# Channel gate of the last image computed from sums inside its last two products, and the first product ahead of the fifth logits

## The chip, the cores and the metric

The kernel runs on one core of one Trainium2 chip. The metric is the device time of one execution in microseconds (us), from the start of the program on the core to its end; of several executions the median is taken. All arithmetic is in float32.

## The reference

The input is x, 16 images of 256 channels and 28x28 pixels. Each image is group-normalised, run through two layers that stand in for 3x3 convolutions, gated per channel, and added to what came in:

```python
def amm_conv3x3(x, centroids, w_sub):
    p = patches of 3x3, per pixel and channel 9 values          # B, HoWo, C, 9
    d = |p|^2 - 2 p.centroids + |centroids|^2                   # 16 centroids a channel
    attn = softmax(-d)                                          # over the 16
    lut = einsum('cks,cso->cko', centroids, w_sub)
    return einsum('bnck,cko->bno', attn, lut)

def se_layer(x, w1, b1, w2, b2):
    s = mean(x, axis=(2, 3))
    s = relu(s @ w1 + b1)
    s = sigmoid(s @ w2 + b2)
    return x * s

xn = groupnorm(x, 32 groups)
out = relu(batchnorm(amm_conv3x3(xn, centroids1, wsub1)))
out = batchnorm(amm_conv3x3(out, centroids2, wsub2))
out = se_layer(out, se_w1, se_b1, se_w2, se_b2)
return x + relu(out + xn)
```

The gate of an image (`se_layer`) needs the mean of each of its 256 output channels over all 784 pixels, so it needs the whole of the second layer's output for that image.

## The kernel before

**Tiling.** Channels lie on the 128 partitions, in two halves. The pixels of an image are cut into two halves of 392 columns (`N`). A block is one layer, one image, one half of the input channels and one half of the pixels: 2 x 16 x 4 = 128 blocks. Each block loads its patches (`patches`, SyncE's queue), multiplies them with the centroids into PSUM (`logits`, 64 matrix products), takes exponentials on ScalarE (`exps`), multiplies these with the centroids' values (`num_b`, which also gives the softmax's denominators, then `num_a`), and scales by the reciprocal denominators (`recip_dve`, `spread`, `scale_a` on VectorE, `scale_q` on GpSimd). What is left per block are nine operands q of 128x392 that meet nine 128x128 weight matrices.

**Products.** The four blocks of an image would need eight products of nine matrices each (two input halves, two output halves, two pixel halves). As in Strassen's scheme they are combined into seven: `PRODUCTS` lists them by the cluster in which they run, `mix` (GpSimd) forms the differences of operands, `combine` those of weights. One product is one call of `product`, nine matrix products of 128x128 by 128x392, each of which the trace shows as two instructions. The outputs land in the regions c11, c12, c21 and c22 (output half, pixel half) by `acc_copy`, `acc_add` and `reg_add`. In image order the products carry the numbers 5 to 12; those that matter here are 9 to 12 of the last image. Product 11 is needed by c11 alone, product 12 by c21 alone.

**Order.** No scheduler sets the order. Every call is entered in a table by `at(cluster, sub, function, ...)`, and the program is recorded in the order of the sorted keys; each engine then runs its instructions in that order and waits where an operand or a buffer is not ready. In the table g is 8 times the number of the image within the two layers (0 to 31, so the second layer's last image has n = 31); a key like (g + 11, 1.9) is a place in the eleventh cluster after that image's first. Blocks overlap: while one block's products run, the next ones' logits, exponentials and scalings run.

**PSUM.** A ring of four tiles of two banks each (tags ps0 to ps3, `banks`, `bank`) serves everything. Which tag a tile gets follows from its step and a role (`ROLES`); for the first blocks a table overrides it (`EARLY`), and a call without step goes round robin. A new tile waits until the last reader of the tile with the same tag is done.

**The start.** Image 0's second half of channels and image 1's normalisation run among the first blocks. Product 5 of image 0 (`acc`, weights w_A) is split: at sub 0.8 five of its nine matrices, then the group means of image 1 (`gn_mean`), two matrices, the group variances (`gn_var`), two matrices. All four logits groups of block 2 stand around it. Image 1 arrives in one transfer (`load_x`).

**The end.** After the last product c21 is formed (`acc_add`), scaled and summed by channel (`norm_out`, ScalarE with an accumulator); then the gate: `se_hidden` (four matrix products, two ScalarE operations), `se_gate` (one matrix product, three ScalarE operations), `se_recip` (VectorE); then `finish_fast` per channel half (two VectorE passes of 784 columns) and `store` (SyncE's queue). `flags` checks, with nine small VectorE operations, that the softmax stayed in range, `flag_sum` adds the flags up on TensorE, and every engine loads the sum at the end; were it above zero, a slower fallback (the loop under `tc.If`) would redo everything. It is not run here. The second last image's gate and output (`finish_gate`, `finish_sum`, `finish_relu`, `finish_add`) run on ScalarE and GpSimd beside the last image's products.

Of the kernel before, what the change touches and what calls it, by code (L numbers as in the profile page):

```python
# [55 lines left out]
    "acc": {4: 0, 6: 1, 7: 3}, "small": {4: 1},  # L56
# [28 lines left out]
def kernel(  # L85
# [83 lines left out]

    def load_x(b, spare=False):  # L170
        if spare:
            t = epool.tile([P, 4, N], F32, tag="e", name="e").rearrange("p i n -> p (i n)")
            t = t.rearrange("p (b n) -> p b n", b=NB)
# [5 lines left out]
    def load_x0(k):  # L179
        if k == 0:  # L180
            xs[0] = io.tile([P, NB, HW], F32, tag="xt", name="xt")
        nc.sync.dma_start(xs[0][:, k], x[0, k * P : (k + 1) * P])

    load_x0(0)
# [46 lines left out]
    load_x0(1)  # L231
# [67 lines left out]
    def small_bank(name, step):  # L299
        return bank(name, step, step and ROLES["small"][step % 2], EARLY["small"].get(step))  # L300
# [42 lines left out]
    def gn_mean(b, k0=0, n=NB, step=None):  # L343
        st, mv = gst[b]
        ps = small_bank("gnp", step)[:, : 2 * n]
# [14 lines left out]
    def gn_var(b, k0=0, n=NB, step=None):  # L360
        gm, dv = gst.pop((b, "m"))
        ps = small_bank("gnp", step)[:, :n]
# [186 lines left out]
    def product(key, us, w, ks, first=True, last=True, step=None):  # L549
        if first:  # L550
            accs[key] = bank("acc", step, step and ROLES["acc"][step % 2], EARLY["acc"].get(step))
        for n, k in enumerate(ks):
            nc.tensor.matmul(  # L553
                accs[key][:, :N], lhsT=wl[w][:, k, :], rhs=us["q", k],
                start=first and n == 0, stop=last and n == len(ks) - 1,
            )
# [282 lines left out]
    def se_hidden(b, step=None):  # L839
        ysum = ys[b, "sum"]  # L840
        ps = small_bank("sep", step)[: 2 * RED, :1]
        terms = [(k, i) for k in range(NB) for i in range(2 if b >= B - 1 else 1)]
        for k, i in terms:
            nc.tensor.matmul(  # L844
                ps, lhsT=w1_sb[:, k, :], rhs=ysum[:, k, i : i + 1],
                start=(k, i) == terms[0], stop=(k, i) == terms[-1],
            )
# [5 lines left out]
    def se_gate(b, step=None):  # L853
        ps = small_bank("sep", step)[:, :NB]
# [16 lines left out]
    def finish_norm(b, k):  # L871
        if k == 0:
            if b == B - 1:
                ys[b, "t"] = epool.tile([P, 4, N], F32, tag="e", name="xn").rearrange("p i n -> p (i n)")
# [25 lines left out]

    def store(b, k, dst=None, eng=None):
# [22 lines left out]
    def flag_sum():  # L924
        ps = bank("flp")[:, :1]
# [76 lines left out]

    for l in range(2):
        for b in range(B):
# [3 lines left out]
            for c, w, r, ks in PRODUCTS:  # L1008
                if g + c == 5:
                    for sub, k0, k1 in ((0.8, 0, 5), (0.82, 5, 7), (0.84, 7, 9)):  # L1010
                        at(4, sub, product, (n, c), us[r], w, ks[k0:k1], k0 == 0, k1 == 9, step=4)
                else:
                    at(g + c, 1.32 if g + c == 7 else 2.0, product, (n, c), us[r], w, ks, step=g + c)
            for mm in (1, 2, 3, 4, 0):
# [3 lines left out]
                at(g + 10, 1.4, mix, us[0], mm, us[0], us[3])  # L1018
# [10 lines left out]
            at(g + 12, 0.0, acc_add, l, b, c11, (n, 11))  # L1029
            at(g + 12, 2.02, acc_add, l, b, c21, (n, 12), op=ALU.subtract)  # L1030
            if l == 0 or b == B - 1:
                at(g + 11, 1.9, norm_out, l, b, *c12)
                at(g + 11, 1.91, norm_out, l, b, *c22)
                at(g + 12, 1.9 if l else 0.05, norm_out, l, b, *c11)
                at(g + 13, 1.06, norm_out, l, b, *c21)
            else:
                for o in range(NB):
                    at(g + 12 + o, 1.9, norm_both, b, o)
            if l == 0:
# [8 lines left out]
                if b + 1 < B:  # L1048
                    at(*((g - 2 + (b == 1), 2.6 - (b == 1)) if b else (0, 1.65)), load_x, b + 1)
                    for q in range(NB):  # L1050
                        at(*(((g + 1, 1.5) if b == 1 else (g, 0.3)) if b else (3, 1.3)), gn_stats, b + 1, q)
                    at(*((g + 1, 2.1) if b else (4, 0.81)), gn_mean, b + 1, step=g + 1 if b else 4)
                    at(*((g + 3, 2.1) if b else (4, 0.83)), gn_var, b + 1, step=g + 3 if b else 4)
                    for q in range(NB):
                        at(*((g + 4, 1.9) if b else (4, (0.95, 1.055)[q])), gn_apply, b + 1, q)
                        at(*((g + 4, 1.92) if b else (4 + 3 * q, 1.6 + 0.05 * q)), to_home1, b + 1, q)
            else:
                last = b == B - 1
                at(*((g + 11, 0.6) if last else (g + 13, 2.6)), load_x, b, last)
                at(g + 14 - last, 2.1, se_hidden, b, g + 14 - last)  # L1060
                at(*((g + 14, 1.05, se_gate, b, g + 14) if last else (g + 17, 2.1, se_gate, b, g + 17)))
                at(*((g + 14, 1.05) if last else (g + 18, 0.3)), se_recip, b)
                for q in range(NB):
                    at(*((g + 12, 0.4) if last else (g + 19, 1.9)), finish_norm, b, q)
                    if not last:
# [5 lines left out]
                    else:  # L1071
# [254 lines left out]
```

## Time and profile before

| what | us |
|---|---|
| median of three runs | 2622.44 |
| lowest and highest of them | 2621.93, 2623.15 |
| the profiled execution | 2621.02 |
| its span from first to last instruction | 2619.5 |
| TensorE busy in it | 2583.4 |
| mean granted TensorE clock (1 is full speed) | 0.998 |

The profile is of one more execution. Its times are counted from the start of its span, which is some 1.5 us shorter than the time of that execution. PE is TensorE, DVE VectorE, ACT ScalarE, POOL GpSimd, SP SyncE. A row of a timeline gives start, duration, engine, line, operation, tile written and read, shapes and the number of instructions; in brackets, where there is one, the idle time of the engine before it and what ended that.

### The profile page before, as it was taken

How to read it: one execution, taken by the hardware profiler on the slowest of the kernel's cores; microseconds unless marked ns; L12 is line 12 of the kernel's file. 1: busy time of each engine (PE TensorE's matmuls, PEld its weight loads, DVE VectorE, ACT ScalarE, POOL GpSimd, SP SyncE). 2: the span in 40 equal slices, each digit the busy share in tenths (PEclk: the TensorE clock that was granted, in tenths of full speed). 3: DMA queues.
4: the chain of work that ended last, by engine and by line, in shares of the span. 5: the costliest groups of instructions: out<-in, count | busy, mean ns of one | idle time of the engine just before them, and what ended most of it. 6: DMA issues, size and time to landing. Idle time of an engine off the chain costs nothing.

```text
span 2619.5 us, 85666 instructions
## 1 busy us (share of the span) xinstructions
PE 2583.4 (99%) x36984; PEld 1265.0 (48%) x36984; DVE 1761.6 (67%) x3759; ACT 1360.3 (52%) x1879; POOL 1900.5 (73%) x1316
## 2 busy tenths in 40 slices
PE   6999999999999999999999999999999999999997
PEld 2444454444444444444444444444444444444444
DVE  5776656666566665566676767766776767677665
ACT  5444544444444454444445555555555556555553
POOL 3786666766568766677666887878878778878786
PEclk9999999999999999999999999999999999999999
DMA  8556656655555566554664444444444443444441
GB/s 223 157 162 180 196 152 188 169 170 173 155 144 148 168 184 178 166 166 135 179 168 103 112 109 129 119 122 119 103 118 128 126 117 104 117 123 121 117 121 45
DMA packets 217959, 374.37 MB, mean 143 GB/s; under 512 B 29752, under 2 KB 188520, under 8 KB 217576
## 3 DMA queue, kind: packets, MB, share of 16 engines
q1 hardware_dynamic: 211256, 335.24, 48.1%
q0 software_dynamic: 6320, 33.58, 3.6%
q8 instruction: 295, 4.83, 0.8%
q14 instruction: 88, 0.72, 0.1%
HBM read 288.93 MB, written 79.80 MB: 141 GB/s over the span
## 4 chain that ended last, share of the span: by engine, by line
PE 97%; DMA 1%; DVE 1%; POOL 0%; ACT 0%; SPq 0%; issue 0%; DVEq 0%; POOLq 0%; ACTq 0%
PE acc L553 52%; PE lg L418 17%; PE na L469 14%; PE nb L483 14%; DMA wall<-home 0%; DMA pt<-home 0%; PE sep L855 0%; DVE r L511 0%; SPq L404 0%; ACT e L429 0%; POOL qp L562 0%; PE sep L844 0%; DMA home<-xpad 0%; DMA xt<-in_x 0%; DVE rb L526 0%
## 5 line engine op out<-in xcount | busy, mean ns | idle before, releaser
L553 PE MATMUL acc<-qp,wall 128*128 128x392 f32 x3072 | 1096.8, 500 | 0.9 <-DVE qp L545 0.7
L429 ACT ACTIVATE e<-lg 128x784 f32<-128x784 f32 x960 | 737.9, 820 | 635.1 <-PE lg L418 632.2
L562 POOL TENSOR_TENSOR qp<-qp,qp 128x784 f32<-128x784 f32 x512 | 943.5, 1867 | 155.6 <-DVE qp L545 155.1
L553 PEld LDWEIGHTS acc<-qp,wall 128*128 128x128 f32 x3072 | 566.4, 190 | 507.1 <-issue 56.9
L526 DVE STREAM_SHUFFLE rb<-r 128x392 f32<-128x392 f32 x1024 | 551.0, 604 | 0.0
L418 PE MATMUL lg<-pt,wd 32*32 32x392 f32 x16256 | 483.2, 502 | 7.2 <-DMA wall<-home 4.9
L497 DVE SCALAR_TENSOR_TENSOR r<-nb,kst,r 128x392 f32<-128x392 f32 x128 | 80.1, 626 | 458.6 <-ACT r L493 444.1
L545 DVE TENSOR_TENSOR qp<-na,rb 128x784 f32<-128x784 f32 x352 | 333.8, 972 | 59.4 <-PE na L469 48.2
L483 PE MATMUL nb<-e,cwb 64*32 64x392 f32 x8192 | 373.6, 492 | 0.1
L469 PE MATMUL na<-e,cwa 64*32 64x392 f32 x8192 | 373.7, 492 | 0.0
L534 POOL TENSOR_TENSOR qo<-qo,rb 128x392 f32<-128x392 f32 x128 | 132.5, 1035 | 310.2 <-DVE rb L522 309.4
L511 DVE RECIPROCAL r<-r 128x392 f32<-128x392 f32 x128 | 333.2, 2603 | 4.4
L534 POOL TENSOR_TENSOR qp<-qp,rb 128x784 f32<-128x784 f32 x160 | 295.8, 1858 | 3.2 <-ACT hpad L604 0.4
L483 PEld LDWEIGHTS nb<-e,cwb 64*32 64x32 f32 x8192 | 189.5, 107 | 176.6 <-issue 20.8
L469 PEld LDWEIGHTS na<-e,cwa 64*32 64x32 f32 x8192 | 182.2, 106 | 182.4 <-issue 72.9
L418 PEld LDWEIGHTS lg<-pt,wd 32*32 32x32 f32 x16256 | 120.9, 103 | 281.8 <-issue 243.1
L553 PE MATMUL acc<-qp,w_A 128*128 128x392 f32 x512 | 182.7, 499 | 0.0
L493 ACT ACTIVATE r<-nb,kst 128x392 f32<-128x392 f32 x128 | 86.7, 678 | 162.3 <-PE nb L483 162.3
L453 POOL TENSOR_TENSOR z<-z,mx 128x1568 f32<-128x1568 f32 x32 | 91.8, 2869 | 94.8 <-DVE mx L447 94.8
L553 PE MATMUL acc<-qo,wall 128*128 128x392 f32 x384 | 157.8, 493 | 0.0
L539 ACT COPY qp<-na 128x784 f32<-128x784 f32 x160 | 130.0, 812 | 26.2 <-PE na L469 24.4
L553 PEld LDWEIGHTS acc<-qp,w_A 128*128 128x128 f32 x512 | 94.7, 190 | 82.1 <-DVE qp L545 19.8
(159 smaller groups left out, 1642.8 us busy)
## 6 DMA issues: line engine op xcount, KB each, us to landing
pt<-home SPq DMA_DIRECT2D x762, 209.0 KB
pt<-home SPq DMA_DIRECT2D x762, 104.5 KB
home<-xpad SPq DMA_DIRECT2D x30, 899.0 KB
xt<-in_x SPq DMA_DIRECT2D x30, 784.0 KB
out_dram<-y SPq DMA_DIRECT2D x32, 392.0 KB
d_wS<-st SPq DMA_DIRECT2D x12, 192.0 KB
wall<-d_wS SPq DMA_DIRECT2D x4, 576.0 KB
wall<-in_ws SPq DMA_DIRECT2D x3, 576.0 KB
```

What stands on the lines that cost most here:

```text
L418: nc.tensor.matmul(bk[32 * c : 32 * c + 32, :N].rearrange("p (r w) -> p r w", w=W), lhsT=wts["wd", u["hh"]][32 * i : 32 * i + 32, mm, c, : ...
L429: nc.scalar.activation(eg[:, 2 * i : 2 * i + 2, :], bk[:, :, :N], AF.Exp, scale=2.0)
L453: nc.gpsimd.tensor_tensor(zk, zk, mx.unsqueeze(2).to_broadcast([P, N // 4, K]), ALU.subtract)
L469: nc.tensor.matmul(bs[32 * i : 32 * i + 32, r, :N], lhsT=wts["cwa", u["hh"]][64 * r : 64 * r + 64, mm, i, :], rhs=es[64 * r : 64 * r + 64, ...
L483: nc.tensor.matmul(bs[32 * i : 32 * i + 32, r, :N], lhsT=wts["cwb", u["hh"]][64 * r : 64 * r + 64, mm, i, :], rhs=es[64 * r : 64 * r + 64, ...
L511: nc.vector.reciprocal(u["r"], u["r"])
L526: nc.vector.stream_shuffle(rb[:, r, :], u["r"], mask_of(2 * mm + r))
L534: nc.gpsimd.tensor_tensor(q, q, u.pop(("rb", mm)), ALU.mult)
L539: nc.scalar.copy(pair(u, mm), u.pop(("na", mm))[:, :, :N])
L545: nc.vector.tensor_mul(pair(u, mm), u.pop(("na", mm))[:, :, :N], rb)
L553: nc.tensor.matmul(accs[key][:, :N], lhsT=wl[w][:, k, :], rhs=us["q", k], start=first and n == 0, stop=last and n == len(ks) - 1,)
L562: nc.gpsimd.tensor_tensor(pair(out_u, mm), pair(in0, mm), pair(in1, mm), ALU.subtract)
```

## The change

It has an end part and a start part.

**End, the gate.** The channel sums of the last image that still depend on products 11 and 12 are no longer taken from the products' outputs. A product's sum over columns is the weights times the operands' sums, so `total_act` (ScalarE, accumulators) and `total_dve` (VectorE) sum the nine operands, `total_sub` takes the difference, `weigh` multiplies the eighteen weight matrices of A12 and A22 by these sums (ScalarE, written with a step of nine elements), `weigh_sum` adds them over the nine (VectorE), and `rest_sum` adds over the partitions (two matrix products with one column) and multiplies by the batch norm's scale. `se_hidden` gets two more terms from it. Product 11 is split 5 / 2 / 2 with `rest_sum`, then `se_hidden` and `flag_sum`, between its parts, and `se_gate` follows it, ahead of product 12.

**End, the last product.** Product 12 runs as two halves of 196 columns, in two PSUM tiles (tags 2 and 3). Everything but its contribution is finished beforehand: `norm_join` and `finish_part` for c11, c12 and c22, `finish_ahead` for c21. Each half is then finished by two VectorE operations on 196 columns (`finish_last`) and stored at once, the second from ScalarE's queue.

**End, the second last image.** Its gate and sum run on ScalarE into PSUM tile ps3 (`gate_wide`) and in two VectorE operations (`finish_wide`); its GpSimd and second ScalarE pass fall away. Image 15's x is loaded earlier and normalised earlier, into the patch tile pt0, which is free by then.

**Start.** Five matrices of product 5 move ahead of block 2's first logits, in a new order (`KO1`). Image 1 arrives by halves of its channels, and each half has its own statistics, group means and group variances: the first half's at the old places, the second half's after block 2.

```diff
-    ("lg", 2): ((1, 0), (3, 2), (3, 2), (1, 0)), ("nb", 2): 3, ("na", 2): (0, 2, 3, 1),
+    ("lg", 2): ((1, 2), (3, 1), (3, 2), (1, 0)), ("nb", 2): 3, ("na", 2): (0, 2, 3, 1),
...
+KO1 = (2, 3, 4, 5, 8, 0, 1, 6, 7)
...
+    def gate_wide(b, k):
+        ys[b, "g"] = banks("gp", tag=3)[:, :, :N]
+        y = ys[b, k].rearrange("p (t n) -> p t n", t=2)
+        nc.scalar.activation(ys[b, "g"], y, AF.Copy, scale=se[b][:, k : k + 1])
...
+    def total_act(u, k):
+        nc.scalar.activation(
+            spare_of(NB * S * P, N, 1), u["q", k], AF.Identity, bias=zero, scale=one, accum_out=qsum[:, 1, k : k + 1]
+        )
...
+    def weigh(o, ks):
+        for k in ks:
+            nc.scalar.activation(
+                spare_of(o * S * P, S * P, 1).rearrange("p (n k) -> p n k", k=S)[:, :, k], wl["A22" if o else "A12"][:, k, :], AF.Copy, scale=qsum[:, o, k : k + 1]
+            )
+
+    def weigh_sum(o):
+        v = spare_of(o * S * P, S * P, 1).rearrange("p (n k) -> p n k", k=S)
+        nc.vector.tensor_reduce(vsum[:, o, :], v, axis=AX.X, op=ALU.add)
+
+    def rest_sum(b, tag):
+        ps = bank("pv", tag=tag)[:, :NB]
+        for o in range(NB):
+            nc.tensor.matmul(ps[:, o : o + 1], lhsT=vsum[:, o, :], rhs=one, start=True, stop=True)
+        ys[b, "rest"] = rest[:, 1]
+        nc.vector.tensor_tensor(rest[:, 1], ps, rest[:, 0], ALU.mult)
...
+    def finish_last(b, key, n0, n1):
+        y, x0 = ys[b, 1][:, n0:n1], xs[b][:, 1, n0:n1]
+        t = ys[b, "t"][:, HW + n0 : HW + n1]
+        nc.vector.scalar_tensor_tensor(
+            y, accs.pop(key)[:, : n1 - n0], rest[:, 2, 1:2], t, op0=ALU.mult, op1=ALU.add
+        )
+        nc.vector.scalar_tensor_tensor(y, y, 0.0, x0, op0=ALU.max, op1=ALU.add)
...
     def flag_sum():
-        ps = bank("flp")[:, :1]
+        ps = bank("flp", tag=2)[:, :1]
...
-                    for sub, k0, k1 in ((0.8, 0, 5), (0.82, 5, 7), (0.84, 7, 9)):
-                        at(4, sub, product, (n, c), us[r], w, ks[k0:k1], k0 == 0, k1 == 9, step=4)
+                    for sub, k0, k1 in ((0.05, 0, 5), (0.8, 5, 7), (0.82, 7, 9)):
+                        at(4, sub, product, (n, c), us[r], w, KO1[k0:k1], k0 == 0, k1 == 9, step=4)
+                elif n == 2 * B - 1 and c == 11:
+                    for sub, k0, k1 in ((1.95, 0, 5), (1.97, 5, 7), (1.99, 7, 9)):
+                        at(g + c, sub, product, (n, c), us[r], w, ks[k0:k1], k0 == 0, k1 == 9, tag=0)
...
+                elif n == 2 * B - 1 and c == 12:
+                    at(g + c, 1.99, open_last, n)
+                    for h in range(2):
+                        at(g + c, 2.0 + 0.02 * h, product, (n, 12 + h), us[r], w, ks, cols=(N // 2 * h, N // 2 * h + N // 2))
...
+                at(g + 11, 1.96, rest_sum, b, 1)
+                at(g + 11, 1.98, se_hidden, b, None, 1)
+                at(g + 11, 1.995, se_gate, b, None, 1)
...
-                    at(g + 11, 1.9, flags)
-                    at(g + 12, 2.9, flag_sum)
+                    at(g + 11, 1.962, flags)
+                    at(g + 11, 1.985, flag_sum)
```

TensorE, the first product and the logits of block 2, before:

```order
13 L483 MATMUL nb<-e,cwb_151 32x392 x32
14 L418 MATMUL lg<-pt_168,wd_153 32x392 x32
15 L553 MATMUL acc<-qp_175,w_A_141 128x392 x2
16 L553 MATMUL acc<-qp_176,w_A_141 128x392 x2
17 L553 MATMUL acc<-qp_177,w_A_141 128x392
18 L346 MATMUL gnp<-gn_mv,gmat 128x4
19 L553 MATMUL acc<-qp_177,w_A_141 128x392
20 L553 MATMUL acc<-qo_186,w_A_141 128x392
21 L363 MATMUL gnp<-gn_dv,gmat 128x2
22 L553 MATMUL acc<-qp_174,w_A_141 128x392 x2
```

The same place after:

```order
13 L486 MATMUL nb<-e,cwb_151 32x392 x32
14 L556 MATMUL acc<-qp_175,w_A_141 128x392 x2
15 L556 MATMUL acc<-qp_176,w_A_141 128x392 x2
16 L556 MATMUL acc<-qo_186,w_A_141 128x392
17 L421 MATMUL lg<-pt_168,wd_153 32x392 x32
18 L556 MATMUL acc<-qp_174,w_A_141 128x392 x2
19 L349 MATMUL gnp<-gn_mv,gmat 128x2
20 L556 MATMUL acc<-qp_177,w_A_141 128x392 x2
21 L366 MATMUL gnp<-gn_dv,gmat 128x1
```

The logits now stand behind five of the product's matrices, and the two `gnp` products carry one channel half each; those of the second half stand some rows further on, around the first quarter of the next `num_a`.

VectorE, the flags and what follows them, before (`ok`, `fl` and `csum` belong to `flags`, `y<-acc,y` and `y<-y,acc` are `acc_add` of products 11 and 12):

```order
1706 L914 TENSOR_SCALAR ok<-wsum 128x128
1707 L915 TENSOR_SCALAR ok<-wsum 128x128
1708 L916 TENSOR_REDUCE fl<-ok 128x1
1709 L917 TENSOR_SCALAR fl<-fl 128x1
1710 L918 TENSOR_SCALAR csum<-csum 128x2
1711 L919 TENSOR_REDUCE fl<-csum 128x1
1712 L920 TENSOR_SCALAR fl<-fl 128x1
1713 L921 TENSOR_TENSOR fl<-fl 128x1
1714 L922 MEMSET fl 128x1
1715 L590 TENSOR_TENSOR y<-acc,y 128x392
1716 L592 TENSOR_TENSOR y<-y,acc 128x392
1717 L927 COPY fi<-flp 1x1
```

The same place after, behind the two `weigh_sum` and the second part of `rest_sum`:

```order
1722 L1015 TENSOR_SCALAR ok<-wsum 128x128
1723 L1016 TENSOR_SCALAR ok<-wsum 128x128
1724 L1017 TENSOR_REDUCE fl<-ok 128x1
1725 L1018 TENSOR_SCALAR fl<-fl 128x1
1726 L1019 TENSOR_SCALAR csum<-csum 128x2
1727 L1020 TENSOR_REDUCE fl<-csum 128x1
1728 L1021 TENSOR_SCALAR fl<-fl 128x1
1729 L1022 TENSOR_TENSOR fl<-fl 128x1
1730 L1023 MEMSET fl 128x1
1731 L911 TENSOR_TENSOR gp<-gp,xn 128x2x392
1732 L912 TENSOR_SCALAR y<-gp,xt 128x784
1733 L1028 COPY fi<-flp 1x1
```

Between the flags and the copy of their sum (`fi<-flp`) now stands the second half of the second last image's `finish_wide` (`gp<-gp,xn` and `y<-gp,xt`), and the `acc_add` of products 11 and 12 are gone; `norm_join`, `finish_part`, `finish_ahead` and `finish_last` follow.

TensorE at the end, after (`pv` is `rest_sum`, `sep` the gate; before, products 11 and 12 were whole and the gate stood behind both):

```order
1947 L556 MATMUL acc<-qp_180,wall_140 128x392
1948 L954 MATMUL pv<-one,pt_169 128x1 x2
1949 L556 MATMUL acc<-qp_180,wall_140 128x392
1950 L556 MATMUL acc<-qo_188,wall_140 128x392
1951 L849 MATMUL sep<-ysum,w_sb 32x1 x4
1952 L849 MATMUL sep<-rest,w_sb 32x1 x2
1953 L1027 MATMUL flp<-fl 1x1
1954 L556 MATMUL acc<-qp_181,wall_140 128x392 x2
1955 L857 MATMUL sep<-se_hh,w_sb 128x2
1956 L556 MATMUL acc<-qp_182,wall_140 128x196 x2
```

The row `flp<-fl` puts the flag sum inside product 11, and the first half of product 12 (128x196) goes into the PSUM tile that `flp` used.

More of the change, by code (lines that the diff above doesn't have):

```diff
@@ L297, with small_bank @@
     cst = const.tile([P, 64], F32, name="cst")
-    def small_bank(name, step):
-        return bank(name, step, step and ROLES["small"][step % 2], EARLY["small"].get(step))
+    def small_bank(name, step, tag=None):
+        return bank(name, step, step and ROLES["small"][step % 2], EARLY["small"].get(step) if tag is None else tag)
     def center_sq(wf, c0, w, eng=None):
@@ L837, with se_hidden @@
     se = {}
-    def se_hidden(b, step=None):
+    def se_hidden(b, step=None, tag=None):
         ysum = ys[b, "sum"]
[L841 to L847, printed above, removed]
+        ps = small_bank("sep", step, tag)[: 2 * RED, :1]
+        terms = [(k, ysum[:, k, i : i + 1]) for k in range(NB) for i in range(2 if b >= B - 1 else 1)]
+        if (b, "rest") in ys:
+            terms += [(k, ys[b, "rest"][:, k : k + 1]) for k in range(NB)]
+        for n, (k, term) in enumerate(terms):
+            nc.tensor.matmul(ps, lhsT=w1_sb[:, k, :], rhs=term, start=n == 0, stop=n == len(terms) - 1)
         hid = small.tile([2 * RED, 1], F32, name="se_hid")
@@ L1057 @@
             else:
                 last = b == B - 1
[L1059 to L1062, printed above, removed]
+                near = b == B - 2
+                at(*((g + 7, 0.6) if last else (g + 13, 2.6)), load_x, b, last)
```

172 lines of the change are left out of this document (136 added, 36 removed).

## The prediction

> **What bounds the kernel now.** I read the page first, then the chain of waits near both ends, then the timelines of the engines there.
>
> ```profile
> PE 2583.4 (99%) x36984; PEld 1265.0 (48%) x36984; DVE 1761.6 (67%) x3759; ACT 1360.3 (52%) x1879; POOL 1900.5 (73%) x1316
> PE 97%; DMA 1%; DVE 1%; POOL 0%; ACT 0%; SPq 0%; issue 0%; DVEq 0%; POOLq 0%; ACTq 0%
> ```
>
> TensorE is busy 2583.4 of 2619.5 us and is 97% of the chain that ends last. Only the 36 us in which it isn't busy can be won without taking products away, and the change takes none: its places are the end and the first 80 us. The recorded order is the same for all the blocks between, so I put nothing there.
>
> The chain's last part shows what the end costs:
>
> ```profile
> 2587.67 17.98 PE acc L553 x54
> ...
> 2605.74 0.57 DVE y L592
> ...
> 2606.34 0.81 ACT y L608 x2
> ...
> 2609.34 0.18 DVE se_gt L865
> ...
> 2609.55 1.05 DVE y L896
> ...
> 2612.57 0.98 DVE y L899
> ```
>
> and SyncE's row of the timeline, the last that the profile shows at all:
>
> ```profile
> 2613.61 0.33 SPq L902 DMA_DIRECT2D out_dram<-y  x1
> ```
>
> Products 10, 11 and 12 run back to back, 17.98 / 3 = 5.99 us each; product 12 starts at 2605.65 - 5.99 = 2599.66 and ends at 2605.65. Then come c21, its sum, the gate, and four VectorE passes of about 1 us, to 2613.55: 7.9 us in which TensorE has nothing of weight to do. From there to the span's end are another 5.95 us, with one transfer issue and the engines' exits.
>
> **The end, step by step.** How soon can product 12 start, if the gate's sums come first? Two rows set the beginning:
>
> ```profile
> 2581.19 4.19 PE L553 MATMUL acc<-qp,wall 128*128 128x392 f32 x12 [0.65 <-DVE qp L545]
> ...
> 2582.86 0.60 DVE L526 STREAM_SHUFFLE rb<-r 128x392 f32<-128x392 f32 x1
> 2587.39 1.04 DVE L590 TENSOR_TENSOR y<-acc,y 128x392 f32<-128x392 f32 x2 [3.94 <-PE acc L553]
> ```
>
> Product 9 gets another PSUM tile, so its wait of 0.65 for a scaling can fall: start 2580.55, end some 6.1 later, product 10 from 2586.95, product 11 from 2592.95. VectorE is free at 2583.4 and gets five sums. Their price, and those of the other new operations, from rows of like shape:
>
> ```profile
> L447 DVE TENSOR_REDUCE mx<-z 128x98 f32<-128x1568 f32 x32 | 56.8, 1776 | 0.0
> L652 DVE TENSOR_REDUCE pk<-c 128x16 f32<-128x144 f32 x2 | 0.8, 401 | 0.1
> L647 DVE TENSOR_REDUCE cmean<-c 128x9 f32<-128x144 f32 x2 | 0.6, 293 | 0.0
> ...
> 2594.48 0.71 ACT L608 ACTIVATE y<-y,bnsh,bnsc 128x392 f32<-128x392 f32 x1 [2.16 <-DVE y L590]
> 2595.20 0.70 ACT L608 ACTIVATE y<-y,bnsh,bnsc 128x392 f32<-128x392 f32 x1
> 2595.89 1.96 ACT L877 ACTIVATE xn<-e,nrm 128x784 f32<-128x784 f32 x2
> 2608.57 0.41 ACT L858 ACTIVATE se_gt<-sep,nb_sb 128x1 f32<-128x1 f32 x2 [0.47 <-PE sep L855]
> ```
>
> A reduction takes 1.776 us for 1568 columns and 0.293 for 144, so about 0.97 for 784 and 1.35 for 1152. Four pairs and one single are 4.4 us; with the two additions of product 9 between them (1.04) they end near 2588.8 and the second last image's reciprocal near 2589.0. ScalarE's nine sums at 0.72 apart (two L608 rows, 2594.48 and 2595.20) are 6.5 us, done in time. Then `gate_wide`, 0.95, to 2589.95, and the eighteen `weigh`. None of that shape is in the trace. Spacing is 0.15 us for one column (0.41 for two L858, 0.26 each) and 0.94 for 784 (1.96 for two L877, 1.03 each), so a straight line gives 0.28 for 128. Bounds: 0.15 and, from the L608 pair, 0.72. I take 0.28, since 128 columns lie nearer to one column than to 784, and allow 0.38 (the step of nine elements at the price at which L652, which reads with a step, stands to L647, 0.401 to 0.293). 18 x 0.28 = 5.0, to 2595.0; the last reduction, 1.35, to 2596.35; the two one-column products and the multiplication, some 0.6, to about 2597. TensorE meets `rest_sum` behind 10 of product 11's 18 instructions, at 2592.95 + 3.3 = 2596.3, and waits 0.4 or so there. Queued behind it are the rest of product 11 and all of product 12.
>
> By the Trainium skill ("SBUF — State Buffer", Specifications (TRN2)) a line is 16 bytes and each access that crosses to a new one pays a penalty; a step of 36 bytes does so at every element, which speaks against `weigh`'s layout. It names no price for ScalarE and no row here shows such a write; at 0.38 the sum would get at most 0.4 worse, for the reason in the next step.
>
> The flags follow on VectorE. Here they are before, with GpSimd beside them:
>
> ```profile
> 2594.37 1.28 DVE L914 TENSOR_SCALAR ok<-wsum 128x128 f32<-128x128 f32 x1
> ...
> 2597.18 1.19 DVE L918 TENSOR_SCALAR csum<-csum 128x2 f32<-128x2 f32 x1
> ...
> 2598.79 1.38 DVE L921 TENSOR_TENSOR fl<-fl 128x1 f32<-128x1 f32 x1
> 2600.11 0.56 DVE L590 TENSOR_TENSOR y<-acc,y 128x392 f32<-128x392 f32 x1
> ...
> 2591.92 3.64 POOL L562 TENSOR_TENSOR qp<-qp,qp 128x784 f32<-128x784 f32 x2
> 2595.53 1.01 POOL L560 TENSOR_TENSOR qo<-qo,qo 128x392 f32<-128x392 f32 x1
> 2596.51 1.84 POOL L562 TENSOR_TENSOR qp<-qp,qp 128x784 f32<-128x784 f32 x1
> 2598.32 3.65 POOL L883 TENSOR_TENSOR y<-y,xn 128x784 f32<-128x784 f32 x2
> ```
>
> Operations on one or two columns take over 1 us, and each long one ends as a GpSimd instruction ends: L914 at 2595.65 (2595.56), L918 at 2598.37 (2598.35), L921 at 2600.17 (2598.32 + half of 3.65 = 2600.15). So VectorE waits out what GpSimd has running, and the nine take 5.8 us. The change takes L883 and L891 off GpSimd; its last `mix` still ends near 2598.4. Of flags that begin at 2597 the first is held up to there; the others, unhindered, are one on 128 columns at about 0.29 (L647: 0.293 for 144), one on 256 at about 0.41 by the line above, and six on at most four columns at about 0.1: 1.3, ready at 2599.7. That is why up to 1.4 us of a later `weigh` costs nothing.
>
> Behind them on VectorE stand the second `finish_wide` (0.97 + 0.98, like L896 and L899) and then the copy of the flag sum, 0.14. Product 12's first half takes over the PSUM tile that this copy reads, so TensorE, with product 11 done near 2600.8, waits for it to about 2601.85: 2.2 us later than before. Its 36 instructions of half the columns are 5.99 us if they scale:
>
> ```profile
> L553 PEld LDWEIGHTS acc<-qp,wall 128*128 128x128 f32 x3072 | 566.4, 190 | 507.1 <-issue 56.9
> ```
>
> A weight load has a mean of 0.19 us against 0.166 a half pass; were none of it to overlap with the next, the product would take 6.84. Loads run beside products, and I take 6.05: end 2607.9. The gate (two ScalarE steps, one product, three ScalarE steps, 2.1 us between 2607.2 and 2609.34 in the chain above) runs from 2598.5 to about 2602. VectorE then does the join, the reciprocal, two passes of 1 us, three of half and a small one, some 4.4 us, to 2606.2, beside product 12. Only the second half's two operations, 0.65 together as a third of 2.0, remain behind it: 2608.55.
>
> SyncE's last store is now the first half's, near 2607, and the second half's is on ScalarE's queue, so the exit needs less than 5.95 after the last VectorE operation; 5.95 after 2607 would be 2612.9, 5.95 after 2608.55 would be 2614.5. I take 2613.35. **End: 2613.35 - 2619.5 = -6.15 us**, bounds -7.5 (no wait on the flags) and -4 (product 6.84 long, exit at the late value).
>
> **The start.** TensorE's and VectorE's rows that matter:
>
> ```profile
> 50.86 0.89 PE L418 MATMUL lg<-pt,wd 32*32 32x392 f32 x16 [0.96 <-DVE qo L508]
> ...
> 55.55 0.39 PE L346 MATMUL gnp<-gn_mv,gmat 128*128 128x4 f32 x2 [0.31 <-DVE gn_mv L341]
> ...
> 63.48 2.87 PE L483 MATMUL nb<-e,cwb 64*32 64x392 f32 x64
> ...
> 76.58 1.00 PE L418 MATMUL lg<-pt,wd 32*32 32x392 f32 x32
> ...
> 79.52 1.97 PE L418 MATMUL lg<-pt,wd 32*32 32x392 f32 x64 [0.44 <-ACT e L429]
> ...
> 53.13 0.97 DVE L340 BATCH_NORM_STATS2 gn_st<-xt 128x6 f32<-128x392 f32 x2
> 54.14 0.21 DVE L341 BATCH_NORM_AGGREGATE gn_mv<-gn_st 128x2 f32<-128x12 f32 x1
> ...
> 55.97 0.16 DVE L350 COPY gn_gm<-gnp 128x4 f32<-128x4 f32 x1 [0.48 <-PE gnp L346]
> ...
> 60.69 3.62 DVE L545 TENSOR_TENSOR qp<-na,rb 128x784 f32<-128x784 f32 x4
> ...
> 67.17 0.63 DVE L497 SCALAR_TENSOR_TENSOR r<-nb,kst,r 128x392 f32<-128x392 f32 x1 [0.50 <-ACT r L493]
> ...
> 74.78 0.97 DVE L545 TENSOR_TENSOR qp<-na,rb 128x784 f32<-128x784 f32 x1 [0.87 <-PE na L469]
> ```
>
> Putting five matrices of product 5 ahead fills the 0.96, and halved statistics remove the 0.31: TensorE comes to `num_a` 1.3 us earlier. But `num_b` at 63.48 starts when the third L545 of the four that begin at 60.69 is done (60.69 + 3 x 0.9 = 63.4), because it takes that PSUM tile. VectorE gets there by way of the copy at 55.97, which waits for TensorE's `gnp`; in the new order that stands behind the logits and two more matrices, and again comes near 55.6. So I let the 1.3 be lost at `num_b`: 0, bounds -1.3 and 0.
>
> What was taken out comes back. The second half's statistics (two L340 and one L341, 53.13 to 54.27, some 1.15 us) go ahead of the join at 67.17, which has 0.50 of idle time: VectorE is 0.65 later. The shuffles behind it end that much later, and 0.87 of idle time ahead of the L545 at 74.78 hides it. But the second `gnp` product of that half waits for VectorE's part, some 0.7 us, and the last three quarters of `num_a` stand behind it, then the logits at 76.58. The wait of 0.44 at 79.52, for exponentials of those logits, moves with them, or takes up a part. I take +0.5, bounds 0 and 1.2. The second half of image 1 loads behind two weight matrices; TensorE shows no wait for a transfer in these stretches, so nothing is set for that. **Start: +0.5.**
>
> **Sum.** -6.15 + 0.5 = -5.65. The profiled execution, 2621.02, would be 2615.4; it is 1.4 below the median, so the median becomes 2622.44 - 5.65 = **2616.8**. About 0.2%, 5.2 us, can be told from no change: below 2617.2 counts as faster.
>
> **Rivals.**
> (a) The flags stay slow: 5.8 us as before, because VectorE's first ones are held and the others too. Product 12 would start 3.1 later, -3.05 + 0.5 gives 2619.9, within the bound. For it: the rows above. Against: GpSimd has no work left after 2598.4. By the Trainium skill ("SBUF — State Buffer", SBUF: two separate sides) the two engines' shared port pair is an exclusive lock for the whole instruction; the rows agree, and by it nothing is held once GpSimd is done.
> (b) The start keeps its 1.3: if `num_b` isn't held, -6.15 - 1.3 gives 2615.0. Against: the 63.4 above.
> (c) The start costs its 1.2 and the exit is the late one: -5.0 + 1.2 gives 2618.6, within the bound.
> (d) Slower. `weigh` at 1.0 each: a plain element costs 0.001 us (0.94 - 0.15 over 783), and if one of the stepped write costs 6.6 times that, 128 of them and the 0.15 make 1.0. That is 18 us in place of 5, so the sums come 13 late; less the 1.4 of slack, product 12 starts 11.6 later than forecast, and TensorE, which runs in order, has nothing to put there: 2616.8 + 11.6 = 2628.4. At the 0.72 of L608 it would be 2623.4; from 0.67 each there is no gain, from 0.96 a loss over the bound. For it: no row shows such a write. Against: the step of L652 costs only 1.37 times.
> That the gate isn't inside product 11 at all is (a) or (d) in another form: the copy at the end of the flags would be late.
>
> **Chances.** Forecast 0.50, of which 0.40 is below 2617.2 (its own range is 2615.3 to 2618.0); (a) 0.17; (b) 0.16; (c) 0.10; (d) 0.07, of which 0.05 is over the bound. Faster 0.40 + 0.16 = 0.56; within 0.10 + 0.17 + 0.10 + 0.02 = 0.39; slower 0.05. The range takes in (b) and (a): 2614.6 to 2620.6.
>
> **What would show it.** Product 12's first 196 columns start near 2601.9, right behind the copy of the flag sum, and the last VectorE operation ends near 2608.6: that is the end part right. `weigh` in steps of 0.28 to 0.38; flags that end some 1.3 after GpSimd's last `mix`. At the start, `num_b` of block 2 still near 63.4 and TensorE's logits at 76.58 come near 77.2. I am wrong if `num_b` starts near 62.2, if `weigh` spaces over 0.5, or if the span goes on 5.95 us behind the last VectorE operation.

## The result and the profile after

| | us |
|---|---|
| kernel before, median of 15 runs | 2623.15 (2621.12 to 2626.83) |
| changed kernel, median of 15 runs | 2619.0 (2616.78 to 2621.32) |
| ratio, changed to before | 0.9983, 95% interval 0.9976 to 0.9989 |
| profiled execution of the changed kernel | 2619.26, span 2617.7 |

The change saves about 4 us, 0.17% (2.9 to 6.3 us by the interval). The 5.65 us of the forecast lies inside, but that is not how the parts came out: the end gave 6.3, and the start took back some 2 to 3. More runs also put the kernel before at 2623.15 rather than 2622.44. Ratios in this document are taken over the runs and not from the medians, and differ by up to 0.0004 (1 us) from the quotient of the two medians. One execution, of head_only below, ran at a granted clock of 0.609 and took 4029.68 us; no ratio includes it.

To compare profiles I cut each span at one event that all kernels share: the start of the last `num_a`, at 2577.60 us before and at 2582.10 after. From there to the span's end the kernel before needs 41.90 us and the changed one 35.60. Before, the row is:

```profile
2577.60 2.94 PE L469 MATMUL na<-e,cwa 64*32 64x392 f32 x64
```

TensorE's timeline of the changed kernel from that `num_a` on (start, duration, engine, line, operation, tiles, shapes, count, idle time before):

```profile
2582.10 2.94 PE L472 MATMUL na<-e,cwa 64*32 64x392 f32 x64
2584.97 4.22 PE L556 MATMUL acc<-qp,wall 128*128 128x392 f32 x12
...
2600.72 0.66 PE L954 MATMUL pv<-one,pt 128*128 128x1 f32 x4
...
2603.94 0.19 PE L1027 MATMUL flp<-fl 128*1 128x1 f32 x2 [0.67 <-DVE fl L1023]
...
2605.99 2.23 PE L556 MATMUL acc<-qp,wall 128*128 128x196 f32 x12
...
2611.37 0.83 PE L556 MATMUL acc<-qp,wall 128*128 128x196 f32 x4
```

Product 9 no longer waits 0.65 for a scaling. `rest_sum` (`pv`) shows no wait; the flag sum holds TensorE for 0.67. The two half products run their 36 instructions in 6.2 us (2605.99 to 2612.20), where weight loads that overlap with nothing would have needed 6.84; so most of that time does hide.

VectorE, ScalarE and GpSimd in the same stretch:

```profile
2599.59 1.35 DVE L949 TENSOR_REDUCE pt<-pt 128x128 f32<-128x1152 f32 x1 [0.81 <-ACT pt L943]
...
2601.49 0.95 DVE L1015 TENSOR_SCALAR ok<-wsum 128x128 f32<-128x128 f32 x1
2602.37 0.21 DVE L1016 TENSOR_SCALAR ok<-wsum 128x128 f32<-128x128 f32 x1
...
2605.71 0.13 DVE L1028 CAST fi<-flp 1x1 int32<-1x1 f32 x1
...
2612.69 0.36 DVE L996 SCALAR_TENSOR_TENSOR y<-y,pt 128x196 f32<-128x196 f32 x1
...
2594.08 5.48 ACT L943 ACTIVATE pt<-wall,qsum 128x128 f32<-128x128 f32 x18
...
2600.50 1.86 POOL L565 TENSOR_TENSOR qp<-qp,qp 128x784 f32<-128x784 f32 x1
```

Only the first flag operation is held, to 2602.44, where GpSimd's last `mix` ends (2602.36); its twin takes 0.21. The eighteen `weigh` take 5.48 us, 0.30 each. Behind the last VectorE operation the span goes on for 4.65 us, where it was 5.95.

The start, TensorE before and in the changed kernel:

```profile
45.29 2.86 PE L483 MATMUL nb<-e,cwb 64*32 64x392 f32 x64
...
81.45 2.87 PE L483 MATMUL nb<-e,cwb 64*32 64x392 f32 x64
```

```profile
46.39 2.86 PE L486 MATMUL nb<-e,cwb 64*32 64x392 f32 x64
49.19 2.90 PE L556 MATMUL acc<-qp,w_A 128*128 128x392 f32 x8
...
62.79 1.77 PE L421 MATMUL lg<-pt,wd 32*32 32x392 f32 x32 [0.24 <-DVE qp L548]
64.55 2.87 PE L486 MATMUL nb<-e,cwb 64*32 64x392 f32 x64
...
75.93 0.38 PE L366 MATMUL gnp<-gn_dv,gmat 128*128 128x1 f32 x2
76.24 2.21 PE L472 MATMUL na<-e,cwa 64*32 64x392 f32 x48
...
81.02 2.79 PE L421 MATMUL lg<-pt,wd 32*32 32x392 f32 x64
83.74 0.56 PE L486 MATMUL nb<-e,cwb 64*32 64x392 f32 x8
```

The blocks' `num_b` (counted from 0) give the rulers here. From block 1's to block 2's it is 18.2 us before and after, from block 2's to block 3's 17.97 before and 19.19 after. The last `lg` row of 64 takes 2.79 us where the kernel before has 1.97 (the row at 79.52 in the prediction).

### The profile page after: what moved, and what is told of

It is laid out like the page before. It is cut to its first block, busy times and chain, and to the rows that moved or that the text cites. A ratio compares the mean times of both kernels' runs of the same rounds, so it can differ in the third digit from the quotient of the medians.

```text
span 2617.7 us, 85797 instructions
## 1 busy us (share of the span) xinstructions
PE 2589.1 (99%) x37014; PEld 1266.0 (48%) x37014; DVE 1769.6 (68%) x3781; ACT 1371.6 (52%) x1915; POOL 1893.6 (72%) x1313
## 4 chain that ended last, share of the span: by engine, by line
PE 97%; DVE 1%; DMA 0%; ACT 0%; POOL 0%; issue 0%; SPq 0%; DVEq 0%; POOLq 0%; ACTq 0%
PE acc L556 52%; PE lg L421 17%; PE na L472 14%; PE nb L486 14%; DMA pt<-home 0%; DVE rb L529 0%; DVE r L514 0%; PE sep L857 0%; DVE qp L548 0%; ACT e L432 0%; POOL qp L565 0%; PE gnp L366 0%; PE sep L849 0%; DMA xt<-in_x 0%; DVE gn_st L343 0%
## 5 line engine op out<-in xcount | busy, mean ns | idle before, releaser
L556 PE MATMUL acc<-qp,wall 128*128 128x392 f32 (+1 forms) x3088 | 1097.5, 498 | 0.3 <-POOL qp L565 0.2
L548 DVE TENSOR_TENSOR qp<-na,rb 128x784 f32<-128x784 f32 x352 | 333.9, 972 | 59.0 <-PE na L472 47.6
L556 PE MATMUL acc<-qo,wall 128*128 128x392 f32 (+1 forms) x386 | 157.9, 491 | 0.0
L542 ACT COPY qp<-na 128x784 f32<-128x784 f32 x160 | 130.1, 813 | 21.8 <-PE na L472 20.3
```

What stands on the lines that cost most here:

```text
L542: nc.scalar.copy(pair(u, mm), u.pop(("na", mm))[:, :, :N])
L548: nc.vector.tensor_mul(pair(u, mm), u.pop(("na", mm))[:, :, :N], rb)
L556: nc.tensor.matmul(accs[key][:, : cols[1] - cols[0]], lhsT=wl[w][:, k, :], rhs=us["q", k][:, cols[0] : cols[1]], start=first and n == 0, s ...
```

## The experiments

Each kernel's runs stand beside runs of the kernel before on the same chip; the four mid kernels ran on another chip than the rest of the table.

| kernel | end part | order of product 5 | image 1 by halves | ratio to before | 95% interval |
|---|---|---|---|---|---|
| after_again | as changed | new | yes | 0.9988 | 0.9978 to 0.9997 |
| tail_only | as changed | old | no | 0.9974 | 0.9965 to 0.9983 |
| head_only | old | new | yes | 1.0017 | 1.0008 to 1.0027 |
| head_whole | old | new | no | 1.0003 | 0.9994 to 1.0012 |
| head_halves | old | old | yes | 1.0008 | 0.9999 to 1.0018 |
| tail_late_flag | flag sum later | old | no | 0.9991 | 0.9982 to 1.0 |
| tail_flag_mid | copy earlier | old | no | 0.9975 | 0.9965 to 0.9985 |
| mid_none (the same again) | copy earlier | old | no | 0.9976 | 0.9967 to 0.9985 |
| mid_whole | copy earlier | new | no | 0.9971 | 0.9960 to 0.9981 |
| mid_halves | copy earlier | old | yes | 0.9985 | 0.9976 to 0.9994 |
| mid_both | copy earlier | new | yes | 0.9981 | 0.9972 to 0.9990 |

**tail_only**: the change without its start part. Against the changed kernel, in short:

```diff
-    ("lg", 2): ((1, 2), (3, 1), (3, 2), (1, 0))   and "small": {4: 2}
+    ("lg", 2): ((1, 0), (3, 2), (3, 2), (1, 0))   and "small": {4: 1}
-    for sub, k0, k1 in ((0.05, 0, 5), (0.8, 5, 7), (0.82, 7, 9)): product with KO1
+    for sub, k0, k1 in ((0.8, 0, 5), (0.82, 5, 7), (0.84, 7, 9)): product with ks
-    load_half, gn_stats, gn_mean, gn_var per half of image 1
+    load_x(1), gn_stats, gn_mean, gn_var at the old places
```

> The change without its start part. Theory (the start takes back about 1 to 2 us of what the end gives): 6.2 us faster than before, some 1 to 2 us faster than the changed kernel; from the last num_a to the span's end 35.6 us as in the changed kernel (41.9 before), and num_b of block 3 at 81.5 as before, give or take 1 us of scatter at the start. Rival (the start part is worth its 1.3 us, and what is missing of the forecast is lost in the end part): only 3 to 4 us faster than before.

Measured: 2618.98 against 2624.74 us, 5.8 us less; by the ratio, 0.9974, it is 6.8 less (4.5 to 9.2). From the last `num_a` to the end 35.4 us. The end part gives what was forecast, and the rival falls. Against expectation, the start of its profiled execution is slow, though it has nothing new there:

```profile
46.33 2.86 PE L486 MATMUL nb<-e,cwb 64*32 64x392 f32 x64
49.74 0.85 PE L421 MATMUL lg<-pt,wd 32*32 32x392 f32 x5 [0.55 <-DMA pt<-home]
52.19 1.93 PE L421 MATMUL lg<-pt,wd 32*32 32x392 f32 x59 [1.60 <-issue]
...
84.75 1.57 PE L421 MATMUL lg<-pt,wd 32*32 32x392 f32 x32 [1.40 <-DMA pt<-home]
```

From block 1's `num_b` to block 4's it takes 62.7 us, 57.7 before. Waits for patches, and stalls ("issue") in which TensorE waits for nothing the profile shows, come and go between executions. A single profile therefore says little of a microsecond at the start.

**head_only, head_whole, head_halves**: the kernel before with the start part, or one edit of it, in short:

```diff
 head_only, against the kernel before:
-    ("lg", 2): ((1, 0), (3, 2), (3, 2), (1, 0))   and "small": {4: 1}
+    ("lg", 2): ((1, 2), (3, 1), (3, 2), (1, 0))   and "small": {4: 2}
-    for sub, k0, k1 in ((0.8, 0, 5), (0.82, 5, 7), (0.84, 7, 9)): product with ks
+    for sub, k0, k1 in ((0.05, 0, 5), (0.8, 5, 7), (0.82, 7, 9)): product with KO1
-    load_x(1), gn_stats, gn_mean, gn_var at the old places
+    load_half, gn_stats, gn_mean, gn_var per half of image 1
...
 head_whole: without the third pair of lines
 head_halves: without the second pair and the change of ("lg", 2)
```

> The kernel before with the start part alone. Theory: 1 to 2 us slower than before; the first num_b of block 2 starts at the same distance from num_b of block 1 (18.2 us) as before, num_b of block 3 some 1.2 us later. Forecast's own term: 0.5 us slower. Rival (the lead of 1.3 us is kept): 1.3 us faster.

> head_only with image 1 whole: five matrices of product 5 ahead of the logits, one transfer, one set of statistics and group means at the old places. Theory (the cost of the start is the second half's statistics and group products between the first num_a quarter and the rest): no loss against before, num_b of block 3 at the old distance from num_b of block 2 (18.0 us), time within 0.5 us of before. Rival (the new order of logits and product costs it): 1 us slower, like head_only.

> The kernel before with image 1 by halves alone; product 5 stays behind the logits. Theory (the halves, not the order of product and logits, cost the 0.9 to 1.2 us): num_b of block 3 stands 36.9 to 37.3 us behind num_b of block 1 (36.2 before, 36.4 in head_whole, 37.05 in head_only), time 1 us or more above before. Rival (the two together cost it): 36.2 to 36.5, time as before.

Measured: 2628.64, 2624.85 (beside 2624.74) and 2626.55 us (beside 2624.44). By its ratio head_only is 4.5 us slower (2.1 to 7.1), more than theory or rival said; head_whole makes no difference, as expected; head_halves is 2.1 slower, with an interval that just reaches 1. The stretch from block 1's `num_b` to block 3's, however, is 37.05, 36.36 and 36.03 us, 36.17 before. head_halves' rows:

```profile
45.41 2.86 PE L484 MATMUL nb<-e,cwb 64*32 64x392 f32 x64
...
63.03 2.87 PE L484 MATMUL nb<-e,cwb 64*32 64x392 f32 x64
...
74.42 0.38 PE L364 MATMUL gnp<-gn_dv,gmat 128*128 128x1 f32 x2
74.73 2.21 PE L470 MATMUL na<-e,cwa 64*32 64x392 f32 x48
...
81.44 2.87 PE L484 MATMUL nb<-e,cwb 64*32 64x392 f32 x64
```

Halved statistics alone gain 0.58 to block 2 (17.62 against 18.20) and give back 0.44 to block 3 (18.41 against 17.97): the interrupted `num_a` is there. So what I expected of this stretch (36.9 to 37.3) is refuted. The rival had 36.2 to 36.5 and the time as before, and the time is 2.1 us longer: what the halves cost lies elsewhere.

**after_again**: the changed kernel once more.

> The changed kernel once more, beside tail_flag_mid and the kernel before on one chip. Theory (its start part costs 1 to 3 us of what its end part gives): ratio to before 0.9975 to 0.9990, some 2 us above tail_only's 0.9974 and tail_flag_mid. Rival (start part neutral): the same as tail_flag_mid within 0.7 us.

Measured: 2620.41 against 2624.44 us, 0.9988, and 35.7 us from the last `num_a`. Beside tail_flag_mid on the same chip (2618.08) it is 2.3 us slower, as the theory had it; some 0.5 of this is tail_flag_mid's shorter end (35.1). At the start one new wait shows, which depends on the execution:

```profile
49.13 2.87 PE L556 MATMUL acc<-qp,w_A 128*128 128x392 f32 x8 [0.36 <-DMA w_A<-in_ws]
```

**tail_late_flag**: the flag sum after half of product 12.

```diff
-        ps = bank("flp", tag=2)[:, :1]
+        ps = bank("flp", tag=1)[:, :1]
-                    at(g + 11, 1.985, flag_sum)
+                    at(g + 12, 2.005, flag_sum)
```

> tail_only with the flag sum moved from inside product 11 to between the two halves of product 12, in PSUM tile ps1. Theory (product 11 and 12 are held by the flags, 0.7 us at the flag sum and 0.3 at its copy): product 12 starts 0.7 to 1.0 us earlier after the last num_a than the 23.9 of the changed kernel, and the time is 0.5 to 1.0 us below tail_only, unless VectorE, which finishes c11 and c12 beside product 12, ends last then: then the last VectorE operation moves by less than 0.3. Rival (the gate itself is what comes late): product 12 starts at 23.9 as before.

Measured: 2623.27 against 2624.74 us, 4.3 us slower than tail_only where 0.5 to 1.0 less was expected, though product 12 starts as expected, 22.9 us after the last `num_a` (2604.22 - 2581.29) instead of 23.9. TensorE's two rows and VectorE's last:

```profile
2581.29 2.94 PE L472 MATMUL na<-e,cwa 64*32 64x392 f32 x64
...
2604.22 2.26 PE L556 MATMUL acc<-qp,wall 128*128 128x196 f32 x12
...
2609.31 0.14 DVE L1028 CAST fi<-flp 1x1 int32<-1x1 f32 x1
...
2611.27 0.36 DVE L996 SCALAR_TENSOR_TENSOR y<-y,pt 128x196 f32<-128x196 f32 x1
```

VectorE ends 0.6 us earlier than in the changed kernel, relative to that `num_a`, and the span (2620.5) goes on for 8.9 us behind it. Every engine loads the flag sum at its end and branches on it, so the copy at 2609.31 starts a second chain. In the trace's records GpSimd, after its load and branch, runs an instruction called DRAIN for 6.61 us, from 2613.03 to 2619.63; in the changed kernel the same one runs from 2609.18 to 2615.79. From the end of the copy to the end of that DRAIN it is 10.2 and 10.0 us, and 10.4 before. In the changed kernel this chain ends 1.1 us ahead of the records in which SyncE is done (2616.89); in tail_late_flag SyncE is done at 2615.55, and the chain ends 4.1 us behind it. Neither theory had it.

**tail_flag_mid**: the other way, the copy earlier.

```diff
-                    at(g + 11, 1.985, flag_sum)
+                    at(g + 11, 1.992, flag_sum)      # TensorE: behind product 11, ahead of the gate
+                    at(g + 11, 1.993, flag_copy)     # VectorE: ahead of finish_wide's second operation
...
```

Not shown is that finish_wide's second operation becomes a call of its own, which moves behind the copy together with its store.

> tail_only with the flag sum between product 11 and the gate's last product, and its copy ahead of the second finish_wide operation instead of behind it: earlier, not later. Theory (the end has two chains: TensorE, VectorE and the stores on one side, and on the other what the engines do once the flag sum is there, which in the first batch needed 11.2 us from the copy to the end of the span): product 12 starts 23.2 to 23.3 us after the last num_a (23.9 in tail_only), the copy some 0.6 earlier, and from the last num_a to the span's end 34.9 to 35.1 us (35.4 in tail_only, 39.2 in tail_late_flag). Rival (the late copy had nothing to do with the longer exit, any move of the flag sum lengthens it): over 36.

The same two rows of TensorE, and VectorE's:

```profile
2581.70 2.94 PE L472 MATMUL na<-e,cwa 64*32 64x392 f32 x64
...
2604.83 2.23 PE L556 MATMUL acc<-qp,wall 128*128 128x196 f32 x12
...
2604.54 0.14 DVE L1037 CAST fi<-flp 1x1 int32<-1x1 f32 x1 [0.18 <-PE flp L1031]
...
2611.54 0.36 DVE L1000 SCALAR_TENSOR_TENSOR y<-y,pt 128x196 f32<-128x196 f32 x1
```

Measured: product 12 starts 23.1 us after the last `num_a` (2604.83 - 2581.70), and from that `num_a` to the span's end it is 35.1 us (35.2 in mid_none, the same kernel). That is 0.2 to 0.5 less than in the kernels with the later copy (35.4 in tail_only to 35.7 in after_again), no more than the least that was expected. The runs (0.9975 and 0.9976) can't tell it from tail_only. The rival falls.

**weigh_flat**: `weigh` without the step.

```diff
-spare_of(o * S * P, S * P, 1).rearrange("p (n k) -> p n k", k=S)[:, :, k]
+spare_of(o * S * P + k * P, P, 1)
-        v = ....rearrange("p (n k) -> p n k", k=S)
+        v = ....rearrange("p (k n) -> p n k", k=S)
```

> tail_only with weigh written without a step, each 128 columns in a row, and weigh_sum reading with a step of 128 elements instead. Theory (the step of the write is not paid for): the eighteen weigh take 5.4 to 5.5 us as with the step, and the two reductions grow from 1.35 towards 1.8 if a read with a step costs what it cost L652. Rival (the stepped write is penalised): 18 weigh in 5.0 or less.

ScalarE's and VectorE's rows:

```profile
2592.58 5.36 ACT L943 ACTIVATE pt<-wall,qsum 128x128 f32<-128x128 f32 x18
...
2597.97 2.19 DVE L949 TENSOR_REDUCE pt<-pt 128x128 f32<-128x1152 f32 x1
```

Written in a row, the eighteen take 5.36 us, with the step of nine 5.48: a difference of 0.007 us each, and the rival (5.0 or less) falls. Reading with the step costs far more, 2.19 against 1.35 us, where 1.8 was expected. The step is on the cheap side. One profile was taken of it, and its single time, 2617.56, tells no more.

**mid_none, mid_whole, mid_halves, mid_both**: both start edits, one, or none, on tail_flag_mid, on one chip. The edits are those of the head kernels.

> tail_flag_mid once more, as the base of the three that follow: neither start edit. About 6.5 us below the kernel before (0.9975); num_b of block 1 to num_b of block 3 36.2 us if no transfer holds TensorE, last num_a to the end 35.1.

> tail_flag_mid with five matrices of product 5 ahead of the logits, image 1 whole. Theory (the order alone gives and takes nothing): within 0.7 us of mid_none, block 1 to block 3 36.4. Rival (product 5, which now needs w_A earlier, waits for its transfer): 0.4 us or more over mid_none.

> tail_flag_mid with image 1 by halves, product 5 behind the logits. Theory of the traces (block 1 to block 3 takes 36.0, 0.1 less than before): within 0.7 us of mid_none. Rival (the transfer by halves costs time that these stretches do not show, as head_halves and head_only were 2 and 4 us above before): 1.5 us or more over mid_none.

> tail_flag_mid with both start edits, that is the changed kernel with the flag sum moved. Forecast's term for the start: 0.5 us over mid_none, block 1 to block 3 36.7. Theory of the second batch: 1 to 3 us over mid_none, 36.7 to 37.4 there. Against the changed kernel 0.4 us less.

Measured: 2616.33, 2616.36, 2619.28 and 2617.61 us beside 2623.25. The order alone gives and takes nothing, as its theory had it; the halves alone cost 3.0 us over mid_none, as their rival had it (1.5 or more); both edits together cost 1.3, within the 1 to 3 expected, but a third of what head_only showed. With the head kernels there are four pairs that differ in the halves alone: +0.0008 (head_halves to before), +0.0014 (head_only to head_whole), +0.0009 and +0.0010 (the mid kernels); the mean is 0.0010, 2.7 us. Four pairs differ in the order of product 5 alone: +0.0003, +0.0009, -0.0005 and -0.0004, mean 0.0001. In no pair are the two intervals against the kernel before apart, but for the halves all four have one sign. Set beside each other, the medians of these four pairs differ by 2.1, 3.8, 3.0 and 1.3 us, and all but one of head_only's runs lie above the highest of head_whole's (2627.69). So it is the halves that cost, as far as these runs tell; how much varies from pair to pair.

In the stretch itself mid_both takes 36.57 us (18.16 and 18.41), 0.4 more than before, and mid_halves 36.29. But mid_none and mid_whole, without the halves, took 36.44 and 37.16 in their profiles, because the logits just ahead of block 3's `num_b` took longer there: one profile scatters by as much as the term. Part of the rest is found far behind it. In all six profiles with the halves, and in none of the eight without, one logits group just ahead of the `num_b` of block 51, a millisecond into the run, takes 0.5 to 0.8 us longer. mid_halves:

```profile
1044.09 1.71 PE L421 MATMUL lg<-pt,wd 32*32 32x392 f32 x32
...
1345.09 4.11 PE L556 MATMUL acc<-qp,w_A 128*128 128x392 f32 x12 [1.11 <-DVE rb L525]
```

mid_whole, the same group:

```profile
1045.26 0.94 PE L421 MATMUL lg<-pt,wd 32*32 32x392 f32 x32
```

Inside mid_halves' row the weight loads pause for 0.65 us, with no releaser in the profile. The second row of mid_halves, a wait of 1.1 us behind a VectorE shuffle ahead of block 66, stands in the changed kernel's first profile too, and a shorter one (0.8 us more for the block) in mid_both. From block 5's `num_b` to block 127's the six profiles take 2446.4 us in the mean and the eight 2445.1, each kind with a scatter of 2.5 to 3 us; of the 1.35 us between the means 0.64 is block 51 and 0.48 block 66. The instructions there are the same in all kernels. What the halves change for them is the timing of the first 80 us and how many instructions stand ahead: TensorE has 14,842 matrix records ahead of block 51's `num_b` in the six profiles, and 14,838 in the eight.

## Why the prediction was right, and where not

The forecast's end part came true step by step. Times from the start of the last `num_a`:

| step | before | forecast | changed kernel |
|---|---|---|---|
| product 9 starts | 3.59 | 2.95 | 2.87 |
| eighteen `weigh` done | | 17.4 | 17.5 |
| second `weigh_sum` done | | 18.75 | 18.8 |
| flags ready | 22.6 | 22.1 | 21.8 |
| copy of the flag sum done | 28.8 | 24.25 | 23.7 |
| product 12 starts | 22.1 | 24.25 | 23.9 |
| last VectorE operation ends | 35.95 | 30.95 | 30.95 |
| span ends | 41.9 | 35.75 | 35.6 |

- **The number.** 2619.0 us lies inside the range that was given (2614.6 to 2620.6), but above the forecast's own (2615.3 to 2618.0), and it did not come below the 2617.2 that had a chance of 0.56. Of the 2.2 us between it and 2616.8, 0.7 is the kernel before, which more runs put higher; most of the rest is the start. The nearest number is rival (c)'s 2618.6, and that is luck: its late exit did not come (4.65 us), and its 1.2 us for the start was less than the start cost.
- **End, -6.15.** Measured -6.30 (35.60 against 41.90), and -6.8 in runs for tail_only (4.5 to 9.2; 5.8 by the medians). `weigh` was taken at 0.28 and took 0.30; the reductions, at 1.35, took 1.35; the half products, at 6.05, took 6.2; ScalarE's nine sums came 0.87 apart, not 0.72, and were still done in time; the flags were held by GpSimd's last `mix` and not beyond, as said. `pv` cost TensorE no wait that shows (0.4 forecast), the flag sum did (0.67); these change places and the sum stays.
- **The exit**, taken at 4.8 us behind the last VectorE operation, was 4.65. That term was right with half its reason: I saw the stores, and not the chain behind the flag's copy. tail_late_flag shows that this chain would have ruled if the copy had stood 1.1 us later. It is a missing rival.
- **Rival (a)**, slow flags: refuted, the nine took 2.4 us (2601.49 to 2603.89) and not 5.8. **Rival (d)**, stepped writes at 0.67 or more each: refuted, 0.30, and without the step 0.30 too.
- **Start, the lead of 1.3 us.** Lost at `num_b` of block 2, as said: 18.16 us from block 1's in the new order, 18.20 before, with TensorE waiting for the L548 scaling (0.24) ahead of it. Rival (b) falls.
- **Start, +0.5 for the second half.** The logits at 76.58 come 0.7 later, counted from block 1's `num_b` (0.6 forecast), and in its own stretch the sum holds where nothing else intervenes: mid_both 36.57 against 36.17, +0.4; the changed kernel's 37.35 has 0.8 more in one logits group. But as a term for the whole kernel it was mis-sized: the halves cost 2.7 us by the four pairs. The failing step is "The recorded order is the same for all the blocks between, so I put nothing there." The order is the same and the time isn't: block 51 alone takes 0.5 to 0.8 us longer in all six profiles with the halves.
- **The profiled execution** of before, on which the sum was made, was itself a favourable one: 2621.02 against a median of 2623.15. From block 16's `num_b` to block 64's it needed 963.0 us, the fourteen profiles 963.0 to 967.4, and its last `num_a`, at 2577.60, is the earliest of the fourteen (the others 2578.8 to 2585.8).

What stays open: why the logits group ahead of block 51's `num_b` stalls with the halves alone, and what makes up the rest of their 2.7 us. A stall without a releaser that comes with four more matrix records ahead would suit the supply of instructions; no run here shows that supply, and none was tried that adds idle instructions. So it is not shown whether the halves themselves cost, or any edit that lengthens the program there would. Nor were the three edits of the end run apart: what each gives is read from the steps in the table alone.

What beats both the kernel before and the changed one is the end part without the halves: mid_none and tail_flag_mid (0.9976, 0.9975), or mid_whole, which has the new order of product 5 as well (0.9971). The runs can't tell these two kinds apart.

## What to carry to other kernels

Where a last reduction stands between the last product and the output, take it from the operands' sums: the products' sums are linear in them, and they are known a product earlier; eighteen small ScalarE operations and two reductions hid beside products 10 and 11, 6 us each. Value such a part between two events that both kernels share, and value a small edit at the start by the whole time, over many runs: part of what the halves cost stood a millisecond behind the edit, and one profile of the start scattered by more than the edit was worth. What all engines read at the end, a flag or a count, belongs early, since a second chain hangs on it.

## What the runs showed of the hardware that was not expected

- From the copy of the flag sum to the end of GpSimd's exit it is 10.0 to 10.4 us in three kernels, 6.61 of them in one DRAIN; a copy 4.4 us later after the last `num_a` made the exit behind the last VectorE operation 4.2 us longer.
- ScalarE writes 128 float32 with a step of 36 bytes at 0.304 us, and in a row at 0.298. A VectorE reduction of 1152 columns takes 1.35 us when it reads them in a row and 2.19 with a step of 512 bytes. The Trainium skill ("SBUF — State Buffer", Specifications (TRN2)) speaks of a penalty for each access that crosses to a new line of 16 bytes; the read agrees with it, 1.6 times, and the write does not.
- VectorE's reductions of 1152 columns took the 1.35 us forecast from other rows although GpSimd's `mix` ran beside them, while an operation of 128 columns, L1015, took 0.95 us, from 2601.49 to 2602.44, and its twin behind the end of `mix` (2602.36) 0.21.
